# Attention and experts on one core: moved blocks that land on every fourth partition, and transposed tokens stored in that order

## The chip, the cores and the metric

The kernel runs on one core of a Trainium2 chip. The metric is device time in microseconds of one launch, measured several times; the median of three runs of the kernel before is 1260.9 us (1260.34 to 1262.82). The profile is one further execution, which took 1259.97 us; the span from its first to its last instruction is 1258.3 us.

## The reference

All values are float32. Eight batches of 512 tokens with 256 features are normalised; then attention with 16 heads of 64 and a mixture of 16 experts both read the normalised tokens, and their results are added to the input.

```python
xn = _layernorm(x)                                   # x: (8, 512, 256)
qkv = (xn @ qkv_w.T).reshape(B, S, 3, 16, 64)        # q, k, v of 16 heads
q, k = _rope(q, c, s), _rope(k, c, s)
scores = jnp.einsum('bhqd,bhkd->bhqk', q, k) * SCALE
kb = -p * jnp.log1p(a * jnp.abs(pos[None, :] - pos[:, None]))
attn = jax.nn.softmax(scores + kb, axis=-1)
out = jnp.einsum('bhqk,bhkd->bhqd', attn, v) @ out_w.T
# experts: each token goes to its best of 16 experts, 256 places each
h = jax.nn.relu(jnp.einsum('ecm,emf->ecf', dispatched, w1))
expert_out = jnp.einsum('ecf,efm->ecm', h, w2)
y = x + out + gathered * gate
```

## The kernel before

The 16 heads are cut into four groups of four. A *step* is one group on one batch, so there are 32 steps, and a step holds two pairs of heads. A *unit* is one pair and one block of 128 queries (`qc`); the main loop takes two units at a time (a *duo*), so a step has four duos and the kernel 128. The order of instructions on each engine is the order in which the program emits them, written out by hand; no scheduler moves anything.

TensorE's work for a step is: q and k of both pairs (`project_qk`, L574), v (`project_v`, L601), the scores (`score`, L624), attention times values (`attend`, L716) and the output projection (`project_out`, L755). From step 5 to about three quarters of the program the two expert matmuls (L519, L534) are interleaved with it.

The tokens come to these matmuls transposed: `xnT` is 128 partitions (features) by two halves of the features by 512 tokens. For the first four batches it is made in place by `transpose_normed` (transposes on TensorE at L271, copied out of PSUM at L274), for the other four it goes through a temporary tile; all eight are stored to DRAM as `xnd`, and later steps load it back (L239). `logits` (L295) reads the same tile for the router of the experts. `project_qk` streams `xnT` as the moving operand and yields q and k with their features on the partitions and 512 tokens in order along the row; `project_v` takes `xnT` as the stationary operand, 128 tokens at a time, so that token `m` of the slice becomes partition `m` of v.

The scores have the queries on the partitions and the keys along the row; attention times values needs the keys on the partitions. The kernel turns the exponentials in two steps. VectorE transposes blocks of 32 by 32 in place (`turn`, L648). That leaves each block of 32 queries by 32 keys in the partition quadrant of its queries, while it belongs in the place of its keys. `move` brings the blocks there with 16 DMAs for each pair and step, one for each query quadrant `qi` and key group `g`, in the order of `BLOCKS`; each moves 32 rows of 4,096 bytes, 128 KB. In the score tile the keys are already stored as `(g c k)`, where a key's number is `c*128 + g*32 + k`, so that one DMA takes the same group `g` of all four 128-key chunks `c`. Row `k` of group `g` lands at partition `g*32 + k`, the place of key `g*32 + k` of its chunk, which is the partition that v has for it. Softmax's sums travel beside them (`rd`, `rb`, L666 and L669), and `attended` (L726) divides.

All these DMAs are issued by SP's queue, in order, together with the loads of `xnT`, of the expert weights and of the partial outputs. In the program's list of instructions the waits of each SP issue name one of eight counters in turn, DMAHW0 to DMAHW7: an issue waits until the DMA eight places before it has landed.

For the very last pair nothing is moved: `turn_last` (L684) scales the exponentials while it puts the keys back into plain order, and TensorE transposes them (L690).

Of the kernel before, what the change touches and what calls it, by code (L numbers as in the profile page):

```python
# [19 lines left out]
P = 128  # L20
NTOK = B * S
NT = NTOK // P
TB = S // P
# [14 lines left out]
def attention_and_experts(  # L38
# [13 lines left out]
    nc = tc.nc  # L52
# [34 lines left out]
    wg = const.tile([P, 2, 32], F32, name="wg")  # L87
# [119 lines left out]
    def deviations(b0, b1, eng):  # L207
# [23 lines left out]
        else:  # L231
            eng.tensor_tensor(t, mv[:, ns, 0], r, ALU.mult)
            eng.tensor_scalar(off[:, ns], t, -1.0, None, ALU.mult)

    xnTs: dict = {}

    def load_normed(s):
# [22 lines left out]
    def transpose_normed(b, copies=None):  # L260
        xn = xns.pop(b)
        if b < 4:
            xnT = xpool.tile([P, 2, S], F32, tag="xnT", name=f"xnT_{b}")
            xnTs[b] = xnT
        else:
            xnT = early.tile([P, 2, S], F32, tag="xt", name=f"xnT_{b}", bufs=2)
        for mc in range(2):
            pool, tag = ((ps_av, "av"), (ps_mm, "mm") if b == 2 else (ps_po, "po"))[mc]
            pt = pool.tile([P, S], F32, tag=tag, name=f"xt_{b}_{mc}")
            for i in range(TB):  # L270
                nc.tensor.transpose(  # L271
                    pt[:, i * P : (i + 1) * P], xn[:, i, mc * P : (mc + 1) * P], ident
                )
            (copies or (nc.scalar.copy,) * 2)[mc](xnT[:, mc, :], pt)  # L274
        stores.append(lambda: nc.gpsimd.dma_start(xnd[b], xnT))
        xns[b] = xnT

# [11 lines left out]
    def logits(b):  # L289

        xnT = xns.pop(b)
        pl = ps_po.tile([P, P], F32, tag="po", name=f"lgp_{b}")
        for mc in range(2):
            for i in range(TB):
                nc.tensor.matmul(  # L295
                    pl[i * 32 : (i + 1) * 32, :], wg[:, mc, :], xnT[:, mc, i * P : (i + 1) * P],
                    start=(mc == 0), stop=(mc == 1),
                )
        lgT[b] = early.tile([P, P], F32, tag="lgT", name=f"lgT_{b}")
        nc.scalar.copy(lgT[b], pl)  # L300
# [267 lines left out]
    def project_qk(s, pair, part, turn_too=True):  # L568
        g, b = divmod(s, B)
        wq, _ = weights[g]  # L570
        ps = ps_mm.tile([P, S], F32, tag="mm", name=f"qk_{s}_{pair}_{part}")
        c0 = part * GC + pair * P
        for mc in range(2):
            nc.tensor.matmul(  # L574
                ps, wq[:, mc, c0 : c0 + P], xnTs[s][:, mc, :], start=(mc == 0), stop=(mc == 1),
            )
        sh = rope.tile([P, S], F32, tag="sh", name=f"sh_{s}_{pair}_{part}", bufs=3)
        nc.vector.stream_shuffle(sh, ps, ROT)  # L578
        t = qkpool.tile([P, S], F32, tag=f"qk{part}{pair}", name=f"t_{s}_{pair}_{part}")
        qk[s, pair, part] = t  # L580
        if not turn_too:
            return ps, sh, t
        nc.scalar.copy(t, ps)  # L583
        turn_by(nc.gpsimd, t, t, sh, slice(0, S))

    def turn_by(eng, t, ps, sh, c):
        eng.tensor_tensor(t[:, c], ps[:, c], cos_t[:, c], ALU.mult)  # L587
        eng.tensor_tensor(sh[:, c], sh[:, c], sin_t[:, c], ALU.mult)  # L588
        eng.tensor_tensor(t[:, c], t[:, c], sh[:, c], ALU.add)  # L589
# [60 lines left out]
    def move(s, pair):  # L650


        z = zts.pop((s, pair))
        inv = inverse[(2 * s + pair) % 2]
        nc.vector.reciprocal(inv[:, : 2 * TB], sums.pop((s, pair)).rearrange("p j c -> p (j c)"))
        turned = small.tile([P, 32], F32, tag="turned", name=f"turned_{s}_{pair}", bufs=2)
        nc.vector.transpose(turned, inv)
        pt = ptpool.tile([P, TB, TB, 2, P], F32, tag="pt", name=f"pt_{s}_{pair}")
        rd = rdram.tile([TB, 32, 32], F32, tag="rd", name=f"rd_{s}_{pair}")
        for i, (qi, g) in enumerate(BLOCKS):  # L660
            nc.sync.dma_start(  # L661
                pt[g * 32 : (g + 1) * 32, qi].rearrange("p c j q -> p (c j q)"),
                z[qi * 32 : (qi + 1) * 32, g].rearrange("p c j q k -> p (c j q k)"),
            )
            if i == 3:
                nc.sync.dma_start(rd.rearrange("a c q -> (a c) q"), turned)  # L666
        rb = rope.tile([P, TB, P], F32, tag="rb", name=f"rb_{s}_{pair}")
        for j in range(2):
            nc.sync.dma_start(  # L669
                rb[j * D : (j + 1) * D],  # L670
                rd[:, j * TB : (j + 1) * TB, :].rearrange("a c q -> a (c q)").partition_broadcast(D),
            )
        pts[s, pair] = pt
        norms[s, pair] = rb

    def turn_last(s, pair, qc):

        if qc == 0:
            pts[s, pair] = zpool.tile([P, 2, TB, S], F32, tag="z", name=f"pt_{s}_{pair}")
        rs = small.tile([P, 2], F32, tag="rs", name=f"rs_{s}_{pair}_{qc}")  # L680
        nc.vector.reciprocal(rs, sums[s, pair][:, :, qc])
        for j in range(2):
            zn = rope.tile([P, S], F32, tag="sh", name=f"zn_{s}_{pair}_{qc}_{j}", bufs=3)
            nc.vector.tensor_scalar(  # L684
                zn.rearrange("p (c g k) -> p g c k", g=TB, k=32),
                zts[s, pair][:, :, :, j, qc, :], rs[:, j : j + 1], None, ALU.mult,
            )
            ps = ps_mm.tile([P, TB, P], F32, tag="mm", name=f"zt_{s}_{pair}_{qc}_{j}")
            for kc in range(TB):
                nc.tensor.transpose(ps[:, kc, :], zn[:, kc * P : (kc + 1) * P], ident)  # L690
            nc.scalar.copy(pts[s, pair][:, j, :, qc * P : (qc + 1) * P], ps)
# [133 lines left out]
    bias_tables(0, 0, 1)  # L825
    moments(1, (0,))
    transpose_normed(0, (nc.vector.tensor_copy, nc.vector.tensor_copy))
    moments(1, (1,))
    deviations(1, 2, nc.gpsimd)
    q0 = project_qk(0, 0, 0, False)  # L830
    k0 = project_qk(0, 0, 1, False)
    nc.scalar.copy(q0[2][:, 2 * P :], q0[0][:, 2 * P :])
    normalise(1)
# [5 lines left out]
    turn_by(nc.gpsimd, q0[2], q0[2], q0[1], slice(2 * P, S))  # L839
    bias_tables(0, 1, 1)  # L840
    project_qk(0, 1, 0)
    transpose_normed(1)
    k1 = project_qk(0, 1, 1, False)
    turn_by(nc.vector, k1[2], k1[0], k1[1], slice(0, S))
# [8 lines left out]
    for d in range(duos):  # L853
        s, dd = divmod(d, TB)
        g, b = divmod(s, B)
# [4 lines left out]
        if d in turned_at:  # L860
            transpose_normed(turned_at[d])
# [41 lines left out]
        if half and not final:  # L903
            move(s, pair)
# [5 lines left out]
        if d in (0, 2):  # L910
            logits(d // 2)
        if d in turned_at:
            logits(turned_at[d])
# [35 lines left out]
        for bb in range(2):  # L949
            k = d - late - 6 * bb - 4  # L950
# [8 lines left out]
        for bb in (B - 2, B - 1):  # L959
            k = d - duos + 6 - (bb - B + 2)  # L960
# [75 lines left out]
```

## Time and profile before

| | before |
|---|---|
| median of runs | 1260.9 us (1260.34 to 1262.82) |
| profiled execution | 1259.97 us, span 1258.3 us |
| PE busy | 1214.7 us, 97% of the span |
| VectorE, ScalarE, GpSimd busy | 892.5, 611.8, 618.1 us |
| q and k projections (L574) | 512 instructions, 604 ns mean, 246.4 us busy |
| moved blocks (L661) | 1,008 DMAs of 128 KB from SP's queue |
| `xnT` copies out of PSUM (L274) | 14 on ScalarE at 592 ns, 2 on VectorE at 686 ns (medians) |
| last pair's scaled copies (L684) | 8 on VectorE at 484 ns (median) |
| DMA queue of SP | 144,848 packets, 240.98 MB, 72.5% of the 16 engines' time |

A float32 matmul of the program shows as two instructions, each with a weight load: 256 in the program's `project_qk` are 512 in the profile. Instructions overlap in their records, so that a group's count times its mean is more than its busy time; busy time counts a moment once. The time from one start to the next says how fast they follow each other.

### The profile page before, as it was taken

Reading aid. Unit: us, or ns where it says so; the run is one execution under the profiler, and the core shown is the slowest. Engines: PE = TensorE matmul, PEld = TensorE weight load, DVE = VectorE, ACT = ScalarE, POOL = GpSimd, SP = SyncE. Lnnn points to the kernel's source line nnn. Section 1 sums busy time; section 2 is a strip of 40 time slices with the busy share of each in tenths; the row PEclk is TensorE's granted clock in tenths of the full one; section 3 lists DMA queues with packets and bytes.
Section 4 is the critical chain, followed back from the end, with each engine's and each line's share of the span. In section 5 each row is a group of like instructions: output and inputs, shape, how many; then the busy total and the mean of one; then the engine's idle time right before and its main releaser. Section 6 shows DMA issues by size and latency. Waiting matters only on the chain.

```text
span 1258.3 us, 17383 instructions
## 1 busy us (share of the span) xinstructions
PE 1214.7 (97%) x5070; PEld 669.1 (53%) x5070; DVE 892.5 (71%) x2265; ACT 611.8 (49%) x1425; POOL 618.1 (49%) x614
## 2 busy tenths in 40 slices
PE   8799999999999999999999999999999999998977
PEld 5344444444465656656565665655656554444444
DVE  7988899999966656555656566655665668888762
ACT  6565655566443444335543344443446435555550
POOL 5766754555543444334443344433434335687850
PEclk9899999999999999999999999999999999999988
DMA  4489998888888997778786787877778768889995
GB/s 135 146 219 262 253 252 203 207 218 208 212 240 210 239 265 193 198 198 212 199 232 166 237 202 211 227 196 205 195 196 215 191 166 203 220 229 218 246 232 139
DMA packets 152414, 264.15 MB, mean 210 GB/s; under 512 B 32176, under 2 KB 96448, under 8 KB 152320
## 3 DMA queue, kind: packets, MB, share of 16 engines
q1 hardware_dynamic: 144848, 240.98, 72.5%
q0 software_dynamic: 6368, 20.99, 5.8%
q10 hardware_dynamic: 1104, 1.07, 0.2%
q8 instruction: 41, 0.67, 0.2%
q14 instruction: 53, 0.43, 0.1%
HBM read 99.39 MB, written 31.44 MB: 104 GB/s over the span
## 4 chain that ended last, share of the span: by engine, by line
PE 76%; DVE 8%; DMA 7%; SPq 4%; POOL 2%; ACT 2%; issue 1%; ACTq 0%; DVEq 0%; POOLq 0%
PE sc L624 15%; PE qk L574 14%; PE av L716 14%; PE ph L519 9%; PE po L534 9%; PE v L601 7%; PE po L755 7%; SPq L661 3%; DVE z L635 3%; DMA pt<-z 2%; DVE z L648 2%; DMA rd<-turned 1%; DMA xnT<-xnd 1%; DMA xnd<-xnT 1%; DMA out<-early 1%
## 5 line engine op out<-in xcount | busy, mean ns | idle before, releaser
L587 POOL TENSOR_TENSOR t<-t,cos_t 128x512 f32<-128x512 f32 (+1 forms) x126 | 161.3, 1280 | 537.9 <-ACT t L583 537.4
L639 ACT ACTIVATE z<-z,st 128x512 f32<-128x512 f32 x512 | 363.4, 712 | 35.2 <-DVE st L635 26.0
L635 DVE CUSTOM_DVE_ANT_1 z<-sc,kb 128x512 f32<-128x512 f32 x512 | 322.5, 686 | 29.2 <-PE sc L624 23.8
L648 DVE STREAM_TRANSPOSE z<-z 128x512 f32<-128x512 f32 x504 | 319.9, 682 | 0.0
L624 PE MATMUL sc<-t,t 64*128 64x512 f32 x1024 | 254.7, 616 | 0.7 <-DVE t L589 0.7
L574 PE MATMUL qk<-xnT,wq 128*128 128x512 f32 x512 | 246.4, 604 | 6.5 <-ACT early L781 1.9
L716 PE MATMUL av<-pt,v 128*64 128x512 f32 x1008 | 232.1, 602 | 3.7 <-DMA rb<-rd 1.8
L583 ACT COPY t<-qk 128x512 f32<-128x512 f32 x125 | 73.2, 585 | 330.6 <-DVE sh L578 324.3
L624 PEld LDWEIGHTS sc<-t,t 64*128 64x128 f32 x1024 | 88.3, 186 | 154.1 <-issue 124.3
L578 DVE LOAD_MASK_SELECT sh<-qk x128 | 1.8, 14 | 231.6 <-PE qk L574 224.7
L589 POOL TENSOR_TENSOR t<-t,sh 128x512 f32<-128x512 f32 (+1 forms) x126 | 160.6, 1275 | 9.9
L588 POOL TENSOR_TENSOR sh<-sh,sin_t 128x512 f32<-128x512 f32 (+1 forms) x126 | 161.2, 1279 | 0.0
L716 PEld LDWEIGHTS av<-pt,v 128*64 128x64 f32 x1008 | 67.8, 137 | 159.6 <-issue 131.3
L574 PEld LDWEIGHTS qk<-xnT,wq 128*128 128x128 f32 x512 | 93.8, 191 | 95.2 <-issue 67.5
L755 PE MATMUL po<-wo,o 128*128 128x256 f32 x512 | 124.4, 386 | 0.4 <-ACT t L583 0.2
L601 PE MATMUL v<-wq,xnT 128*128 128x256 f32 x512 | 124.1, 385 | 0.0
L534 PE MATMUL po<-w,hT 128*128 128x256 f32 x512 | 120.3, 383 | 1.0 <-ACT hT L525 1.0
L519 PE MATMUL ph<-xdT,w 128*128 128x256 f32 x512 | 118.7, 382 | 1.4 <-ACT eot L540 1.4
L755 PEld LDWEIGHTS po<-wo,o 128*128 128x128 f32 x512 | 94.4, 190 | 36.9 <-issue 12.6
L601 PEld LDWEIGHTS v<-wq,xnT 128*128 128x128 f32 x512 | 94.7, 190 | 35.8 <-DVE z L648 13.8
L519 PEld LDWEIGHTS ph<-xdT,w 128*128 128x128 f32 x512 | 95.7, 190 | 26.5 <-ACT z L639 4.9
L534 PEld LDWEIGHTS po<-w,hT 128*128 128x128 f32 x512 | 95.2, 190 | 25.3 <-issue 8.7
(147 smaller groups left out, 831.9 us busy)
## 6 DMA issues: line engine op xcount, KB each, us to landing
pt<-z SPq DMA_DIRECT2D x1008, 128.0 KB
w<-in_w SPq DMA_DIRECT2D x64, 512.0 KB
rb<-rd SPq DMA_DIRECT2D x126, 128.0 KB
xnT<-xnd SPq DMA_DIRECT2D x28, 512.0 KB
yd<-y SPq DMA_DIRECT2D x26, 512.0 KB
y<-yd SPq DMA_DIRECT2D x24, 512.0 KB
xrd<-xn POOLq DMA_DIRECT2D x8, 512.0 KB
xnd<-xnT POOLq DMA_DIRECT2D x8, 512.0 KB
```

The source lines that it names most:

```text
L519: nc.tensor.matmul(ph[:, i, :], held["w1", e, fc // 4][:, mc, (fc % 4) * P : (fc % 4 + 1) * P], xdT[:, mc, :], start=(mc == 0), stop=(mc = ...
L534: nc.tensor.matmul(po[:, c, :], hT[:, fc, c * P : (c + 1) * P], held["w2", e, fc // 4][:, fc % 4, :], start=(fc == 0), stop=(fc == F // P ...
L574: nc.tensor.matmul(ps, wq[:, mc, c0 : c0 + P], xnTs[s][:, mc, :], start=(mc == 0), stop=(mc == 1),)
L587: eng.tensor_tensor(t[:, c], ps[:, c], cos_t[:, c], ALU.mult)
L588: eng.tensor_tensor(sh[:, c], sh[:, c], sin_t[:, c], ALU.mult)
L601: nc.tensor.matmul(ps[:, i, :], xnTs[s][:, mc, c0 : c0 + P], wq[:, mc, 2 * GC :], start=(mc == 0), stop=(mc == 1),)
L624: nc.tensor.matmul(sc[j].rearrange("p (g c k) -> p g c k", g=TB, k=32), q[r, qc * P : (qc + 1) * P], k[r, :].rearrange("p (c g k) -> p g c ...
L635: nc.vector.tensor_tensor_reduce(z, sc[j].rearrange("p (g c k) -> p g c k", g=TB, k=32), bias, -0.125, 3.0e38, ALU.add, ALU.min, st[:, j : ...
L639: nc.scalar.activation(z, z, AF.Exp, bias=st[:, j : j + 1], scale=-1.0, accum_out=sums[s, pair][:, j, qc : qc + 1],)
L648: nc.vector.transpose(z, z)
L716: nc.tensor.matmul(av[j * D : (j + 1) * D, :].rearrange("p (a q) -> p a q", q=P), vals[s][:, kc, c0 : c0 + D], pts[s, pair][:, :, kc, j, : ...
L755: nc.tensor.matmul(ps[:, i, :], oTs[pair][:, c0 : c0 + P], wot[:, pair, :], start=(pair == 0), stop=(pair == 1),)
```

## The change

Row `k` of key group `g` now lands at partition `4*k + g` instead of `32*g + k`. The order of the keys on the partitions of the moved tile `pt` is thereby another one, and everything that meets it takes the same order: the transposed tokens are stored as `(c k g)`, so v, whose stationary operand is still read in one piece, has its tokens on the same partitions. q, k and the logits keep the plain token order: their matmuls read `xnT` through `in_order`, which walks it as `(c g k)`, that is with a step of four elements (16 bytes) along the innermost 32, while they write PSUM in one piece. The copies out of PSUM that make `xnT` write with the same step, and so do the copies of the last pair. The numbers of instructions, DMAs and bytes, and the order on every engine's queue, are as before.

```diff
+    def in_order(t):
+        return t.rearrange("p (c k g) -> p c g k", g=TB, k=32)
...
-            (copies or (nc.scalar.copy,) * 2)[mc](xnT[:, mc, :], pt)
+            (copies or (nc.scalar.copy,) * 2)[mc](
+                in_order(xnT[:, mc, :]), pt.rearrange("p (c g k) -> p c g k", g=TB, k=32)
+            )
...
-                    pl[i * 32 : (i + 1) * 32, :], wg[:, mc, :], xnT[:, mc, i * P : (i + 1) * P],
+                    pl[i * 32 : (i + 1) * 32, :].rearrange("p (g k) -> p g k", k=32),
+                    wg[:, mc, :], in_order(xnT[:, mc, :])[:, i],
...
-                ps, wq[:, mc, c0 : c0 + P], xnTs[s][:, mc, :], start=(mc == 0), stop=(mc == 1),
+                ps.rearrange("p (c g k) -> p c g k", g=TB, k=32),
+                wq[:, mc, c0 : c0 + P], in_order(xnTs[s][:, mc, :]),
+                start=(mc == 0), stop=(mc == 1),
...
-                pt[g * 32 : (g + 1) * 32, qi].rearrange("p c j q -> p (c j q)"),
+                pt[g::TB, qi].rearrange("p c j q -> p (c j q)"),
...
-                zn.rearrange("p (c g k) -> p g c k", g=TB, k=32),
+                zn.rearrange("p (c k g) -> p g c k", g=TB, k=32),
```

## The prediction

> **What bounds the kernel now.** I read the page's busy times and slices first, then the costliest groups, then the order of time on PE and on SP's queue, then busy time by window at both ends.
>
> ```profile
> PE 1214.7 (97%) x5070; PEld 669.1 (53%) x5070; DVE 892.5 (71%) x2265; ACT 611.8 (49%) x1425; POOL 618.1 (49%) x614
> ...
> PE   8799999999999999999999999999999999998977
> ```
>
> PE is busy 97% of the span, and the slices put nearly all of its idle time at the two ends. Order of time on PE for one step without experts:
>
> ```profile
> 200.09 1.98 PE L574 MATMUL qk<-xnT,wq 128*128 128x512 f32 x4
> 202.01 1.99 PE L624 MATMUL sc<-t,t 64*128 64x512 f32 x8
> 203.92 3.65 PE L716 MATMUL av<-pt,v 128*64 128x512 f32 x16
> 207.51 1.99 PE L601 MATMUL v<-wq,xnT 128*128 128x256 f32 x8
> ```
>
> Each group starts as the one before drains: four q/k matmuls take 1.92 us from start to start, 480 ns each. From 300 to 1030 us PE's waits add up to 2.7 us (1.4 for L519, 1.0 for L534, 0.3 for L574). So in the middle a nanosecond more on a PE instruction is one on the end, and a faster transfer is worth nothing. The ends differ:
>
> ```profile
> 31.50:62.90 31.40, 23.14 (x121) 10.94 (x122) 29.86 (x86) 18.37 (x47) 24.49 (x38) 0.87 0.48 146
> ...
> 1132.50:1163.90 31.40, 28.22 (x109) 13.37 (x107) 25.36 (x63) 17.93 (x47) 24.20 (x20) 1.00 0.93 218
> 1163.90:1195.40 31.50, 28.52 (x110) 13.50 (x108) 24.97 (x63) 17.57 (x44) 26.55 (x22) 1.00 0.95 246
> 1195.40:1226.80 31.40, 22.59 (x101) 12.73 (x98) 21.59 (x56) 17.34 (x45) 15.69 (x13) 0.87 0.91 232
> ```
>
> (Columns: the window, its length, busy time of PE, weight loads, DVE, ACT, POOL, then the granted clock, DMA share, GB/s.) In the last three rows the DMA engines are at 0.91 to 0.95 and PE loses 3.2, 3.0 and 8.8 us. What it waits for, in order of time:
>
> ```profile
> 1162.14 3.65 PE L716 MATMUL av<-pt,v 128*64 128x512 f32 x16 [1.33 <-DMA pt<-z]
> 1167.02 1.95 PE L574 MATMUL qk<-xnT,wq 128*128 128x512 f32 x4 [1.23 <-DMA xnT<-xnd]
> ...
> 1194.63 3.65 PE L716 MATMUL av<-pt,v 128*64 128x512 f32 x16 [1.75 <-DMA rb<-rd]
> ...
> 1225.37 1.97 PE L690 MATMUL zt<-ident,zn 128*128 128x128 f32 x8 [5.70 <-ACT pt L691]
> ```
>
> That ACT copy waited 4.4 us for moved blocks. SP's queue at the same time:
>
> ```profile
> 1179.93 11.32 SPq L661 DMA_DIRECT2D pt<-z  x12
> ...
> 1196.88 7.50 SPq L661 DMA_DIRECT2D pt<-z  x12
> ```
>
> Twelve issues take 7.50 us when the queue flows and 11.32 when each waits for the landing of the one eight before. So the kernel is bound by PE, with some 10 us at the end and a few at the start in which moved blocks matter.
>
> [...] 256 program matmuls are 512 instructions, and the step from 256 to 512 columns costs 604 - 385 = 219 ns (L574 against L601), 0.855 ns a column. [...] of 47,040 packets of 4,096 bytes 13,833 take under 165 ns, and the rest have a median of 287.
>
> **The change part by part.** The instruction order is the same on all engines, no wait is added, and nothing is moved past anything.
>
> *q/k projections, 512 instructions.* Same columns, moving operand with a 16-byte step. No row of before reads with such a step, so I bound it. Below: nothing[...]; a gain is excluded, since the same columns stream. Above: [...] 512 x 0.855 = 438 ns more for each, x 512 = 224 us, all on the path. I take nothing, at a chance of about six in ten[...].
>
> *Logits, 128 instructions of 128 columns, four side by side.* A batch of 16 takes 0.58 us (47.04 to 47.62 us). Nothing to 8 x 0.58 = 4.6 us; with the same answer as above.
>
> *Copies that make `xnT`, 16.* Contiguous reads, writes with a 16-byte step. VectorE's rate is (686 - 424)/256 = 1.02 ns a column (L274 against L709), ScalarE's (583 - 254)/384 = 0.86 (L583 against L300). [...] 0.52 us each on VectorE, 0.44 on ScalarE. The two of batch 0 stand before the first q/k (PE waits 0.35 us for them at 15.20): up to 1.0 us. Batch 1's stand before the q/k at 29.41 us (wait 0.17): up to 0.9. Batch 2's before the logits at 59.33 us (wait 6.68): up to 0.9. Later ones lie under 1.92 us of scores between transposes and logits and cost about nothing. Bounds 0 to 2.8 us, carried through the dense middle to the end; I take 1.4.
>
> *v.* Stationary operand in one piece as before: nothing.
>
> *Moved blocks, 1,008 DMAs.* Same rows, bytes and issue time (589 ns median on SP). [...] reads still come from 32 neighbours of `z`[...] a packet stays near 287 ns: gain nothing. That reads are the limit is suggested by the `rb` loads, which write 64 neighbours,[...] in 512-byte packets: 25,101 of 32,272 take 24 to 27 ns[...]. Bounds: if all packets went to 159 ns, the tail's waits on moved blocks (1.33 + 1.75 + 5.70, and 0.66 before L716 at 1208.16) and the 3.1 us that batch 2's copy waits for the store of `xnT` could go, 12.5 us; I would count on 9. [...] I take nothing.
>
> *Last pair's copies (L684), 8 at 484 ns.* They are faster a column than the PSUM copies at 686 and may lose that: 0.2 us each[...]. One or two stand on the chain (1236.56 us): 0.2 to 1.0; I take 0.4. The other four are covered by the wait of 5.70 us.
>
> Sum against the profiled span: 1258.3 + 0 + 0 + 1.4 + 0 + 0.4 = 1260.1. The median of runs lies 2.6 us above this span, which gives 1262.7; with the copies at nothing 1260.9. I say 1262.
>
> **The rivals.**
>
> *Blocks arrive sooner (0.29).* The step is free and the writes were part of the limit. For it: DMA share over 0.9 and SP's stretched issues in the tail. Against: unchanged reads, and a middle that cannot gain. 1258.3 - 9 + 1.4 + 0.4 + 2.6 = 1253.7, say 1253.
>
> *The step halves the moving rate (0.27): the one on the other side.* Its place is L574. 1258.3 + 224 + 4.6 + 3.8 for slow copies, less some 6 us of tail waits that a slower PE hides, + 2.6 = 1487. It decides early: every 1% on L574's 480 ns costs 2.5 us, so 1% already cancels no change. [...]
>
> *A partial penalty (0.13).* An access of, say, one and a half times: 112 us, about 1370; anything from 1275 to 1465.
>
> *No change to speak of (0.31), the forecast:* 1262, its own range 1258 to 1267.
>
> **How the numbers follow.** A difference under 0.2%, 2.5 us, is about what a measurement of this kernel cannot tell from none. The forecast's case gives 0.02 faster, 0.18 within, 0.11 slower; sooner blocks 0.29 faster, of which 0.01 falls within; the two penalties 0.40 slower. Faster 0.30, within 0.19, slower 0.51. Since cases of both signs hold the chance, the range has to reach from sooner blocks to the half rate: 1248 to 1489 leaves out a larger DMA gain (about 0.06) and a penalty above two (about 0.12).
>
> **What would show it.** The group of L574: mean 604 ns and busy 246.4 us unchanged if the step is free; about 1,040 ns and 465 us if it halves. L274: 592 and 686 ns against about 1,030 and 1,200. 4,096-byte packets: median of the slow ones at 287 or near 159, and the DMA queue's 72.5% falling towards 50%. In the tail, twelve L661 issues at 11.32 us or at 7.50, and the 5.70 us wait at L690 gone or not. The prediction is wrong [...] by 10 us if writes held the blocks back.

## The result, and the profile after

The changed kernel takes 1478.5 us (1477.9 to 1479.8, four runs) against 1260.6 us for four runs of the kernel before: 1.172 times as long (95% interval 1.1685 to 1.1748). The single likeliest case of the prediction, 1262 us, did not come; the rival on the other side, that the 16-byte step halves the rate of the moving operand (0.27, 1487 us), did. Line numbers of the changed kernel are up to ten higher: L574 is L582 there, L624 L634, L716 L726, L661 L671.

The page of the changed kernel, busy times, PE's slices, DMA queue of SP and chain:

```profile
PE 1450.5 (98%) x5070; PEld 675.0 (46%) x5070; DVE 903.8 (61%) x2265; ACT 618.9 (42%) x1425; POOL 618.1 (42%) x614
...
PE   8999999999999999999999999999999999999997
...
q1 hardware_dynamic: 144848, 240.98, 56.2%
...
PE 96%; DVE 1%; ACT 1%; DMA 1%; issue 0%; POOL 0%; ACTq 0%
PE qk L582 31%; PE sc L634 16%; PE av L726 15%; PE po L765 8%; PE v L611 8%; PE ph L527 8%; PE po L542 8%; ACT xnT L279 1%; PE lgp L302 1%; PE zt L700 0%; PE xdp L512 0%; DMA xnd<-xnT 0%; DVE zn L694 0%; PE av L715 0%; DVE sh L588 0%
```

The chain was 76% PE before and is 96% PE now, with 31% of the span in one line, the q and k projections, where it was 14%. The groups that the change touches, with the scores beside them, forms kept apart (busy us and mean ns after the first bar, the engine's idle time after the second):

```profile
L582 PE MATMUL qk<-xnT,wq 128*128 128x512 f32 x512 | 483.9, 1079 | 1.1 <-DVE xnT L279 0.7 <-DVE y L770 0.3
L634 PE MATMUL sc<-t,t 64*128 64x512 f32 x1024 | 254.4, 615 | 1.8 <-DVE t L599 1.8
L279 ACT COPY xnT<-xt 128x512 f32<-128x512 f32 x14 | 14.2, 1128 | 1.1 <-DMA xnd<-xnT 1.1
L302 PE MATMUL lgp<-xnT,wg 128*32 128x128 f32 x128 | 8.8, 403 | 5.0 <-ACT z L649 3.0 <-ACT xnT L279 2.0
```

The same groups in the kernel before:

```profile
L574 PE MATMUL qk<-xnT,wq 128*128 128x512 f32 x512 | 246.4, 604 | 6.5 <-ACT early L781 1.9 <-ACT t L583 1.6 <-DVE y L760 1.3
L624 PE MATMUL sc<-t,t 64*128 64x512 f32 x1024 | 254.7, 616 | 0.7 <-DVE t L589 0.7
L274 ACT COPY xnT<-xt 128x512 f32<-128x512 f32 x14 | 7.5, 594 | 3.1 <-DMA xnd<-xnT 3.1
L295 PE MATMUL lgp<-xnT,wg 128*32 128x128 f32 x128 | 5.7, 296 | 6.7 <-ACT xnT L274 6.7
```

L582 went from 604 to 1,079 ns and from 246.4 to 483.9 us of busy time; the scores beside it, which read k in runs of 32 neighbours, stayed (616 to 615 ns). In order of time four projections now take 3.69 us from start to start where they took 1.92:

```profile
250.67 3.76 PE L582 MATMUL qk<-xnT,wq 128*128 128x512 f32 x4
254.36 1.99 PE L634 MATMUL sc<-t,t 64*128 64x512 f32 x8
```

The span's 218.5 us more are 235.8 us more of PE busy time, less 17.3 us of PE idle time, 26.3 us instead of 43.6. Of the groups, L582 has 237.5 us more, the logits 3.1 more and the transposes of L276 2.3 less; groups overlap in their records, so they do not add up exactly. Waits of PE on moved blocks are gone: its idle time before L726 is 0.0 us, where before L716 it was 3.7. Two windows near the end, columns as in the prediction:

```profile
1371.40:1402.80 31.40, 31.40 (x98) 11.43 (x98) 23.32 (x59) 15.81 (x40) 22.35 (x19) 1.00 0.78 240
1402.80:1434.30 31.50, 31.50 (x114) 13.28 (x111) 24.66 (x61) 18.96 (x49) 24.04 (x20) 1.00 0.69 202
```

Two questions are left: is it the step, and what in it; and did the landing do anything that the step hides?

### The profile page after: what moved, and what is told of

It is laid out like the page before. It is cut to its first block, busy times and chain, and to the rows that moved or that the text cites. A ratio compares the mean times of both kernels' runs of the same rounds, so it can differ in the third digit from the quotient of the medians.

```text
span 1476.8 us, 17349 instructions
## 1 busy us (share of the span) xinstructions
PE 1450.5 (98%) x5070; PEld 675.0 (46%) x5070; DVE 903.8 (61%) x2265; ACT 618.9 (42%) x1425; POOL 618.1 (42%) x614
## 4 chain that ended last, share of the span: by engine, by line
PE 96%; DVE 1%; ACT 1%; DMA 1%; issue 0%; POOL 0%; ACTq 0%
PE qk L582 31%; PE sc L634 16%; PE av L726 15%; PE po L765 8%; PE v L611 8%; PE ph L527 8%; PE po L542 8%; ACT xnT L279 1%; PE lgp L302 1%; PE zt L700 0%; PE xdp L512 0%; DMA xnd<-xnT 0%; DVE zn L694 0%; PE av L715 0%; DVE sh L588 0%
## 5 line engine op out<-in xcount | busy, mean ns | idle before, releaser
L582 PE MATMUL qk<-xnT,wq 128*128 128x512 f32 x512 | 483.9, 1079 | 1.1 <-DVE xnT L279 0.7
L634 PE MATMUL sc<-t,t 64*128 64x512 f32 x1024 | 254.4, 615 | 1.8 <-DVE t L599 1.8
L726 PE MATMUL av<-pt,v 128*64 128x512 f32 x1008 | 231.4, 601 | 0.0
L634 PEld LDWEIGHTS sc<-t,t 64*128 64x128 f32 x1024 | 88.1, 186 | 265.0 <-issue 228.0
L582 PEld LDWEIGHTS qk<-xnT,wq 128*128 128x128 f32 x512 | 98.9, 200 | 205.4 <-issue 180.4
L598 POOL TENSOR_TENSOR sh<-sh,sin_t 128x512 f32<-128x512 f32 (+1 forms) x126 | 161.5, 1282 | 0.0
L726 PEld LDWEIGHTS av<-pt,v 128*64 128x64 f32 x1008 | 67.0, 137 | 155.8 <-issue 128.5
```

The costliest lines, as they stand in the source:

```text
L582: nc.tensor.matmul(ps.rearrange("p (c g k) -> p c g k", g=TB, k=32), wq[:, mc, c0 : c0 + P], in_order(xnTs[s][:, mc, :]), start=(mc == 0), ...
L634: nc.tensor.matmul(sc[j].rearrange("p (g c k) -> p g c k", g=TB, k=32), q[r, qc * P : (qc + 1) * P], k[r, :].rearrange("p (c g k) -> p g c ...
L726: nc.tensor.matmul(av[j * D : (j + 1) * D, :].rearrange("p (a q) -> p a q", q=P), vals[s][:, kc, c0 : c0 + D], pts[s, pair][:, :, kc, j, : ...
```

## The experiments

Two theories are tested. *Step:* what costs is a step of 16 bytes or more from each single element of the moving operand to the next, and it is all that costs. Its rivals: any step costs, or the walk over runs of 32; or the cost grows with the distance. *Landing:* blocks that land four apart come sooner. Its rivals: reads hold them back, so the landing brings nothing; or packets are faster only because a slower PE thins the traffic.

### The step alone

```diff
-                ps, wq[:, mc, c0 : c0 + P], xnTs[s][:, mc, :], start=(mc == 0), stop=(mc == 1),
+                ps.rearrange("p (c g k) -> p c g k", g=4, k=32),
+                wq[:, mc, c0 : c0 + P],
+                xnTs[s][:, mc, :].rearrange("p (c k g) -> p c g k", g=4, k=32),
+                start=(mc == 0), stop=(mc == 1),
```

> The kernel before with one edit: the q and k projections read the plain transposed tokens with the step of 16 bytes; landing, copies and logits as before. q and k come out in another token order, so the result is another one; the amount of work is the same. If the step alone makes the loss: L574 near 1,079 ns and about 225 us of the 218 us net, total 1470 to 1480. If the loss needs the new landing or the new copies too: clearly below 1450. Packets of 4,096 bytes with the old landing at this slower pace: if only the slower pace made them faster in the changed kernel, some 30,000 are under 165 ns here too; if the landing did it, about 14,000 as before.

Measured: 1470.7 us (two runs), 1.164 times the kernel before (1.1585 to 1.1703). The group of L574:

```profile
L574 PE MATMUL qk<-xnT,wq 128*128 128x512 f32 x512 | 483.8, 1079 | 0.7 <-DVE xnT L274 0.3 <-DVE y L763 0.3
```

The same 1,079 ns as in the changed kernel: the step alone makes practically all of the loss. Some 8 us are left to the changed kernel, but the intervals of the two ratios overlap. The profile of the changed kernel shows where these 8 us can lie: a batch of logits takes 1.03 us from start to start against 0.57 here, some 3.7 us in eight batches, and PE waits 2.0 us for stepped copies before the logits of three later batches, which it does not here. PE waits for no moved block in this run either, with the old landing; its wait for the ACT copies of the last pair (L694 here), 5.9 us in the kernel before, is 0.5 us. Yet the packets of 4,096 bytes are as slow as before: 13,271 under 165 ns. So the slower PE hides slow blocks without making them faster, and the 30,074 fast packets of the changed kernel are the landing's work.

### A step of 8 bytes, pairs, and a step of 64 bytes

Three more kernels change the same place. The first reads with a step of 8 bytes (`g=2, k=32` and eight `c`), the second reads pairs of neighbours with 16 bytes from pair to pair, the third has a step of 64 bytes. By the step theory the first two stay near the kernel before, and the third comes near the run with 16 bytes. PSUM is written in one piece each time:

```diff
+                xnTs[s][:, mc, :].rearrange("p (c k g) -> p c g k", g=2, k=32),
...
+                xnTs[s][:, mc, :].rearrange("p (k h g) -> p h k g", h=2, g=2),
...
+                xnTs[s][:, mc, :].rearrange("p (k g) -> p g k", g=16, k=32),
```

> As the run with the 16-byte step, but with a step of 8 bytes: [...] the innermost run is again of 32 elements. The result is another one, the amount of work the same. [...] L574 stays near 604 ns and the time near 1261. If any step, or the walk over runs of 32, is what costs: near 1,079 ns and 1475 us.

> The kernel before with q and k projections that read two neighbouring elements (8 bytes), then go on by 16 bytes: every second pair, and the others in a second pass. The result is another one, the amount of work the same. [...] L574 near 604 to 624 ns and 1258 to 1275 us[...]. If [...] very short innermost runs do: between 650 and 1,079 ns.

> The kernel before with a step of 64 bytes in the q and k projections, innermost runs of 32 again; the result is another one, the amount of work the same. [...] L574 near 1,079 ns, as with 16 bytes, 1465 to 1480 us. If the cost grows with the step: above 1,300 ns.

These are single runs: 1271.9, 1269.4 and 1451.4 us. They are read by the durations of their 512 instructions. The group of L574 in the three, 8 bytes first:

```profile
L574 PE MATMUL qk<-xnT,wq 128*128 128x512 f32 x512 | 257.4, 624 | 12.5 <-DMA xnT<-xnd 10.4 <-ACT t L586 1.5 <-DVE xnT L274 0.3
```

Pairs:

```profile
L574 PE MATMUL qk<-xnT,wq 128*128 128x512 f32 x512 | 256.1, 622 | 10.6 <-ACT z L642 4.9 <-DMA xnT<-xnd 3.6 <-ACT t L586 1.5
```

64 bytes:

```profile
L574 PE MATMUL qk<-xnT,wq 128*128 128x512 f32 x512 | 462.4, 1036 | 0.7 <-DVE xnT L274 0.3 <-DVE y L763 0.3
```

The step of 8 bytes and the pairs cost 18 to 20 ns on 604; the step of 16 bytes costs 475 and the step of 64 bytes 432. The 8-byte run walks the same runs of 32 as the 16-byte one, so the walk is not it; the pairs go over the row twice, in two passes, and are still cheap (622 ns); and 64 bytes cost slightly less than 16, so between these two the cost does not grow with the distance. The step theory stands, and these two rivals fall. A third was not tested: in the runs that stayed cheap, successive reads start at most 12 bytes apart (but for a jump at the end of each run of 32 or each pass), and in the slow ones 16 or 64. So whether every jump of 16 bytes or more costs, or only elements that are read one by one between such jumps, is not shown; a run of pairs that lie further apart would decide.

### The landing without the step

Two kernels keep the landing and let TensorE read in one piece. The first is the changed kernel with the plain reads of before in L582 and L302. The second finds another place for the new order: GpSimd's last addition of the rotation stores k in it, `xnT` stays plain, v and q are untouched. In it `t` is a spare tile `kt` for k, and only the sum goes to k's own tile.

```diff
+        if part:
+            turned_k[id(sh)] = t
+            t = rope.tile([P, S], F32, tag="kt", name=f"kt_{s}_{pair}", bufs=1)
...
+        if id(sh) in turned_k:
+            eng.tensor_tensor(
+                turned_k.pop(id(sh)).rearrange("p (c g k) -> p c k g", g=TB, k=32),
+                t.rearrange("p (c k g) -> p c k g", g=TB, k=32),
+                sh.rearrange("p (c k g) -> p c k g", g=TB, k=32), ALU.add,
+            )
...
-        dist, pattern=[[32, TB], [P, KBW // P], [1, 32]], base=-(S - P),
+        dist, pattern=[[1, TB], [P, KBW // P], [4, 32]], base=-(S - P),
...
-                pt[g * 32 : (g + 1) * 32, qi].rearrange("p c j q -> p (c j q)"),
+                pt[g::TB, qi].rearrange("p c j q -> p (c j q)"),
...
-                zn.rearrange("p (c g k) -> p g c k", g=TB, k=32),
+                zn.rearrange("p (c k g) -> p g c k", g=TB, k=32),
```

> The changed kernel with its projections and logits reading the transposed tokens in one piece, which leaves q, k and logits in another token order (the result is another one, the amount of work the same). Left of the change are the landing four apart, the stepped copies and the stepped copies of the last pair. If landing four apart brings the blocks sooner: about 1252 to 1256 us, the waits on moved blocks in the last 100 us mostly gone, SP's stretched groups of twelve issues near 7.5 us. If it does not: 1261 to 1264, above the kernel before by the slower copies (0.52 us each, some 2 us in all).

> The kernel before with the landing four apart, made consistent at another place: k is stored in the order of the landing by GpSimd's last operation of the rotation (64 of its 1,280 ns additions write with a step), the table of distances follows, and the last pair's copies are the changed kernel's. TensorE reads what it read before, the transposed tokens are plain. The result is the reference's. If the landing helps: 1250 to 1256 us; if it does not: 1260 to 1262. If GpSimd's stepped write is so slow (over 5 us each) that k comes late, clearly more, with PE waiting before L624.

> The run with k stored in the landing's order by GpSimd once more, for its interval against the kernel before: 0.988 to 0.993 of it, 1249 to 1253 us.

Measured: the first kernel takes 1251.2 us, 0.991 of the kernel before (0.9877 to 0.9942); the second 1250.7 us, 0.990 (0.9867 to 0.9934), and measured again 1249.8 us, 0.9886 (0.9865 to 0.9908). All three intervals lie below 1: the landing gains 11 to 13 us once TensorE is left alone, and the second kernel is faster than both of the case. The stepped copies, which only the first has, cost nothing that shows between the two. Windows of the second kernel near the end, and its order of time on PE:

```profile
1132.50:1163.90 31.40, 31.40 (x123) 14.25 (x120) 27.47 (x71) 20.52 (x52) 25.97 (x21) 1.00 0.83 251
1163.90:1195.40 31.50, 31.50 (x122) 14.50 (x123) 27.57 (x69) 19.38 (x50) 28.72 (x24) 1.00 0.81 247
```

```profile
1189.55 3.65 PE L728 MATMUL av<-pt,v 128*64 128x512 f32 x16
...
1216.80 1.97 PE L702 MATMUL zt<-ident,zn 128*128 128x128 f32 x8 [1.64 <-ACT pt L703]
```

PE lost 3.2 and 3.0 us in these windows before and loses nothing, and in the next one 5.2 us in place of 8.8; DMA share fell from 0.93 and 0.95 to 0.83 and 0.81. The wait of 1.75 us before attention times values and 4 of the 5.70 us before the last pair's transposes are gone. On SP's queue (who waited for whom, total us, times, longest), the issues of moved blocks waited for an `xnT` load 15 times in the kernel before, first fence, and 6 times here; for DMAs of any kind they waited 72.1 us in 59 waits before, and 11.4 us in 19 here:

```profile
SPq L661 <- DMA xnT<-xnd: 22.5, 15, 2.5
SPq L661 <- DMA w<-in_w: 12.1, 9, 2.0
```

```profile
SPq L673 <- DMA xnT<-xnd: 4.6, 6, 1.1
SPq L673 <- DMA w<-in_w: 2.8, 3, 1.0
```

The groups of twelve issues in the last 100 us still take 7.5 to 10.3 us, where they took 7.5 to 11.3; that sign of sooner blocks came only in part.

A variant of the second kernel lets GpSimd read both inputs with the step and write in one piece:

```diff
-                turned_k.pop(id(sh)).rearrange("p (c g k) -> p c k g", g=TB, k=32),
-                t.rearrange("p (c k g) -> p c k g", g=TB, k=32),
-                sh.rearrange("p (c k g) -> p c k g", g=TB, k=32), ALU.add,
+                turned_k.pop(id(sh)).rearrange("p (c g k) -> p c g k", g=TB, k=32),
+                t.rearrange("p (c k g) -> p c g k", g=TB, k=32),
+                sh.rearrange("p (c k g) -> p c g k", g=TB, k=32), ALU.add,
```

> As the run with k stored in the landing's order, with GpSimd's addition reading both inputs with the step of 16 bytes and writing in one piece, where that run writes with the step and reads in one piece; the result is the reference's. If GpSimd reads stepped rows as fast: 1,280 ns and 1250 us, a second measure of landing four apart with TensorE's reads untouched. If stepped reads cost half again as much: 62 additions near 1,900 ns, with GpSimd at half load, still hidden: 1250 to 1252 us.

Measured: 1251.5 us, 0.9931 (0.9910 to 0.9952). The additions of k, writing with the step and then reading with it, and before them q's plain addition in the run that writes with the step:

```profile
L601 POOL TENSOR_TENSOR t<-t,sh 128x512 f32<-128x512 f32 x63 | 80.7, 1282 | 4.9
L595 POOL TENSOR_TENSOR t<-kt,sh 128x512 f32<-128x512 f32 x62 | 79.9, 1289 | 4.9
```

```profile
L595 POOL TENSOR_TENSOR t<-kt,sh 128x512 f32<-128x512 f32 x62 | 132.1, 2130 | 4.9
```

The stepped write (128 bytes from element to element) costs next to nothing on GpSimd, 1,289 against 1,282 ns; the stepped reads cost 0.85 us each, more than was expected, and GpSimd, busy for 54% of the span, hides them.

### What of the landing

Three kernels move blocks of the same size from and to other partitions; they compute another result and serve only to compare. They are landing on every second partition of one half, reading from every fourth, and both sides on every fourth. For the first, two outcomes were named: none of the landing's gain, or about all of it.

```diff
+                pt[g // 2 * 64 + g % 2 : g // 2 * 64 + 64 : 2, qi].rearrange("p c j q -> p (c j q)"),
...
+                z[qi::TB, g].rearrange("p c j q k -> p (c j q k)"),
...
+                pt[g::TB, qi].rearrange("p c j q -> p (c j q)"),
+                z[qi::TB, g].rearrange("p c j q k -> p (c j q k)"),
```

> The kernel before with the blocks landing on every second partition of one half (64 partitions), in place of 32 neighbours; v keeps its order, so the attention sums mix other keys (the result is another one), the amount of work is the same. [...] no gain here, 1258 to 1264 us, about 14,000 packets under 165 ns. [...] near 1250 us and about 30,000.

> The kernel before with the mirror of the landing: each DMA reads its 32 rows from every fourth partition of z and writes 32 neighbours. The moved blocks hold other values (the result is another one), sizes and numbers are the same. If reads hold the blocks back, as the prediction took it: the gain of the changed landing or more, 1245 to 1252 us, 30,000 or more packets of 4,096 bytes under 165 ns. If writes do: no gain, 1258 to 1264 us, about 14,000 packets. [...]

> The kernel before with both sides of each moved block on every fourth partition (the result is another one, sizes and numbers the same). If reading from neighbours is what leaves half of the packets slow after the changed landing: nearly all packets at 159 ns, the DMA queue near 50%, 1243 to 1250 us. [...]

The table has the times, SP's queue share, and from the trace's packet records the 47,040 packets of 4,096 bytes: how many took under 165 ns, the median of the others, how many took 350 ns or more, and their time summed and divided by 16 engines. Each ratio is against the kernel before as measured with that run.

| reads from | lands on | time us, ratio (interval) | queue | under 165 | others, median ns | 350 or more | packets, us |
|---|---|---|---|---|---|---|---|
| neighbours | neighbours (before) | 1262.1 to 1263.0 | 72.5% | 13,833 | 287 | 1,840 | 729 |
| neighbours | every second of a half | 1259.1, 0.9984 (0.9967 to 1.0000) | 69.1% | 23,249 | 278 | 5,485 | 687 |
| neighbours | every fourth (k in new order) | 1250.7, 0.9901 (0.9867 to 0.9934) | 66.0% | 31,454 | 313 | 6,074 | 648 |
| every fourth | neighbours | 1264.4, 1.0012 (0.9991 to 1.0033) | 77.1% | 14,475 | 302 | 10,661 | 769 |
| every fourth | every fourth | 1248.3, 0.9881 (0.9852 to 0.9910) | 55.5% | 31,744 | 168 | 1,144 | 520 |

Spreading the reads alone gains nothing and makes packets slower (its profiled execution took 1270.6 us, above its median); the 512-byte packets, nearly all of them of `rb`, become slower too: 13,843 of them take 24 to 27 ns where 25,101 did. Spreading the writes alone gains nearly all the time there is to gain. Spreading the reads as well leaves as many packets under 165 ns, but the others drop to a median of 168 ns; these 128 us less of packet time are worth only some 2 us, within the intervals, because PE no longer waits in these windows:

```profile
1132.50:1163.90 31.40, 31.40 (x118) 14.42 (x120) 27.46 (x68) 19.49 (x50) 25.99 (x21) 1.00 0.74 250
1163.90:1195.40 31.50, 31.50 (x126) 15.52 (x127) 27.53 (x71) 18.81 (x47) 28.72 (x24) 1.00 0.74 252
```

Landing on every second partition of a half gives half of the packet gain (687 us, with 729 for neighbours and 648 for every fourth), between the two outcomes expected; in time it gains 0.2% as measured, with an interval that reaches 1.0000. What it is in the landing that shortens the packets is not shown by these runs. Which engine takes which row is not in the trace, and why some packets become longer than 350 ns where only one side is spread (5,485 to 10,661 of them, with 1,840 before) stays open.

## Why the prediction was right or wrong

The range held the time, and more than half of the chance, 0.51, stood on slower. But the range was made to reach from sooner blocks to the half rate, and the forecast itself, 1262 us, was off by 216.5 us: its sum failed at its largest term.

*q/k projections: taken as nothing, bounded at 224 us.* Wrong choice, right bound. That the step would cost nothing, at six in ten, was the author's estimate, and no row of the profile showed it. The runs show the contrary: with the step of 16 bytes a mean instruction took 1,079 ns, with 64 bytes 1,036, with 8 bytes or pairs 624 or 622; what it is in the step that costs is left open above. The size was close: 475 ns for a mean instruction and 237.5 us of busy time, against 438 and 224.

*The rival's other terms.* Logits 3.1 us of busy time against 4.6. Copies: ScalarE 1,112 ns median against 592, VectorE 1,080 against 686, so 0.52 and 0.39 us more where 0.44 and 0.52 were given (512 columns more, each at the rate of before). Their waits lay in part elsewhere: the logits of later batches, where they were to cost about nothing, waited 2.0 us for them. Tail waits that the slower PE hides: 6 us taken, but PE's idle time fell by 17.3 us in all, a part of it at the start, where the wait of 6.68 us before the logits of batch 2 became one of 3.0 us, for another releaser. That 1487 was only 8 us too high is partly luck: L574 was taken 13.5 us too low, and idle time, copies included, 15 us too high.

*Moved blocks: taken as nothing, "reads are the limit".* Wrong as the first limit. Spread reads alone gained nothing (1.0012) and spread writes gained 11 to 13 us; only once the writes are spread do spread reads shorten packets (648 to 520 us, where alone they went from 729 to 769). The argument from the 512-byte packets of `rb` did not carry over to blocks of 4,096-byte rows. The rival's price of 9 us was low and the ceiling of 12.5 us of the right size, though not by its parts: the 3.1 us for which batch 2's copy waits for the store of `xnT` stayed (3.7 us in the kernel with k in the new order), and 1.6 of the 5.70 us stayed too. One reading was off as well: in the twelve issues of 11.32 us the trace records waits of 2.3 and 0.7 us, for two loads of partial outputs, not one before each issue. In the changed kernel the landing has nothing to gain: the run with the step alone shows that with the old landing and a slow PE no moved block is waited for either.

*Last pair's copies: 0.2 us each, one or two on the chain, 0.4 us.* The runs with the landing have medians of 686 to 692 ns where 484 were, so 0.2 us each is right. In the changed kernel one of the eight took 2,723 ns; no copy of the other runs with the same step did (724 ns at most), so the step does not explain it, and the cause stays open.

*Dense middle, end ruled by PE.* Right: the loss is the growth of PE's busy time, less the idle time that went. In the middle (300 to 1030 us) PE waits 3.2 us with the new landing and k in the new order, where it waited 2.7, so faster blocks gained nothing there.

*The point from which the rival decides* ("every 1% on L574's 480 ns costs 2.5 us") was the number to weigh. A term that can be 224 us and can't be negative is not balanced by a chance of six in ten for nothing when the other terms are about 1 us.

## What to carry to other kernels

Where TensorE sets the time, let a float32 moving operand be read in one piece, in pairs or with a step of 8 bytes (604, 622 and 624 ns a mean instruction here), not with a step of 16 (1,079; no other type was run), and pay for an order in a place with slack: here a stepped write of GpSimd, at 1,289 ns in place of 1,282. An access pattern that no row of the profile shows can still be bounded from the rows that are there (224 us here, where 237.5 came): price every instruction that reads so at its bound before weighing the chances. A change of two halves is worth splitting: the landing alone is a gain of 1%, nothing of it shows beside a loss of 17%, and a kernel with the one and without the other runs in 1250 us.

## What the runs showed of the hardware that was not expected

- In this kernel the writing side of SBUF-to-SBUF moves of 32 rows was the one to spread first: spreading only the writes took 80 us off the packets' time over 16 engines (729 to 648), spreading only the reads added 40 (769), and spreading both took off 209 (520).
- A step of 64 bytes in the moving operand was slightly cheaper than 16 (1,036 against 1,079 ns, the 64 bytes in a single run).
- GpSimd's float32 addition of 128x512 took 1,289 ns when it wrote with a step of 128 bytes and 2,130 ns when it read both inputs with a step of 16.
- Copies from PSUM that write SBUF with a step of 16 bytes took 1,112 instead of 592 ns on ScalarE and 1,080 instead of 686 on VectorE.
